# A row of attention scores spread by way of DRAM instead of by TensorE, in a four-layer graph network on one core

## The chip, the core and the metric

The kernel runs on one core of a Trainium2 chip. The time is the device time of the program in microseconds (us), the median of several runs. Names of engines: PE is TensorE (PEld its weight loads), DVE is VectorE, ACT is ScalarE, POOL is GpSimd, SP is SyncE, which here only issues transfers.

## The reference

There are 32 graphs with 512 nodes of 256 features, and an adjacency matrix of 512 x 512 for each. Four layers follow one another; each normalises x, applies a relu, runs one kind of graph attention and adds the result to x. Layers 1 and 2 are the ones that matter here. In both, the score of a pair of nodes is a sum of two numbers, one for each node:

```python
h = maximum(layernorm(x), 0)
# layer 1                                     # layer 2
Wh  = h @ W.T                                 Hh = h @ W
src = Wh @ a1 ; dst = Wh @ a2                 s = Hh @ a_src ; d = Hh @ a_dst
e = leaky_relu(src[:, None] + dst[None, :])   e = exp(-leaky_relu(s[:, None] + d[None, :]))
e = where(adj > 0, e, -9e15)                  e = where(adj != 0, e, 0)
x = x + softmax(e) @ Wh                       x = x + elu(e @ Hh / rowsum(e))
```

Layer 0 has scores q h^T and two products with the attention matrix, layer 3 a full bilinear score. Their code is not touched.

## The kernel before

A graph's 512 nodes lie as four tiles of 128 partitions (NT = 4, P = 128), its 256 features as two halves (HC = 2). Attention matrices are held transposed, in the tile eT: the node that is attended to (j) in the partitions, the node that attends (i) along the row, so that a product with the values needs no further transpose.

In layers 1 and 2, `scored_values` computes the values of each tile t and the two scores of its nodes in one product on PE (L488, with two extra columns of weights). DVE copies the two scores into sd (L492) and ACT the values into v (L495). Node t * 128 + p then has its scores in sd[p, 0, t] and sd[p, 1, t]. `leaky_exp_t` builds eT: it needs the first score of all 512 nodes as a row, the same row in every partition. It gets it with four transposes on PE (L509), one for each tile: the column sd[:, 0, t], broadcast over 128 columns and turned, is a block of 128 columns of row, which is one bank of PSUM. ACT then adds the second score as a bias and applies the leaky relu (L513, four times), and the exponential (L517, four times). DVE masks (L649 in layer 1, L684 in layer 2), and `attend` multiplies with the values on PE (L536).

At the start of a layer, `normed` normalises (DVE L407, GpSimd L414, ACT L421), splits the bits into planes (DVE L427), turns the planes with DMA transposes on SyncE (L432), and ACT joins the result to hT (L436), the operand of L488 and of the feature products L463. SyncE also loads x (L193) and adj (L200) and turns the codes made from adj (L389) and a small tile of layer 3 (L753). GpSimd stores the result (L833).

The order of all of this is written out beforehand by the class `Plan`. Every operation is entered with an engine, a cost (how long it holds its engine, and when its result is there), what it waits for, and the places that it takes or reads (8 banks of PSUM, a few buffers). `order` plays the graphs through on these costs: an engine that is free takes, of its ready operations, the one with the lowest rank. The rank is the number of the graph times a distance, less the length of the chain still ahead inside the graph. The distance is `APART` for all graphs, and for the last two steps between graphs `APART_LAST`. The instructions are emitted in the order that comes out, and every engine's queue runs in that order. Four graphs are in flight (`FLIGHT` = 4): graph b uses the tiles of graph b - 4 and begins when that one has been stored.

The tile row takes a bank. The tiles fa, zT and r share one buffer in each slot, one after another: fa and zT in layer 0, r in layer 2, fa again in layer 3.

Of the kernel before, what the change touches and what calls it, by code (L numbers as in the profile page):

```python
# [11 lines left out]
F32 = mybir.dt.float32  # L12
# [3 lines left out]
AF = mybir.ActivationFunctionType  # L16
# [3 lines left out]
P = 128  # L20
EPS = 1e-5
ALPHA = 0.2
# [10 lines left out]
def pe(n512=0, n256=0, nt=0):  # L33
    t = n512 * PE512 + n256 * PE256 + nt * PET
    return t, t + 170.0
# [4 lines left out]
A_COPY, A_HALF, A_PRELU, A_EXP, A_TANH = (477.0, 597.0), (253.0, 373.0), (570.0, 693.0), (519.0, 640.0), (373.0, 474.0)  # L40
A_BIAS, A_PRELU2 = (570.0, 687.0), (629.0, 722.0)
G_POW, G_STORE = (800.0, 850.0), (900.0, 900.0)
A_NORM, A_JOIN, V_SPLIT = (491.0, 590.0), (620.0, 767.0), (332.0, 422.0)
D_TURN = (1310.0, 2600.0)
D_X, D_ADJ, D_ADJ0 = (550.0, 5000.0), (550.0, 12000.0), (550.0, 2500.0)
G_LOAD = (800.0, 5000.0)


class Plan:
# [5 lines left out]

    PASS = 200.0

    APART, APART_LAST = 40000.0, 10000.0
    SLACK = {"V": (1.05, 0.0), "A": (1.05, 0.0), "G": (1.5, 0.0), "D": (1.0, 800.0)}

    def __init__(self):
# [2 lines left out]
    def op(self, engine, cost, after, emit, graph, takes=(), reads=()):  # L64


        much, more = self.SLACK.get(engine, (1.0, 0.0))
        cost = cost[0] * much, cost[1] * much + more
        flat = []
        for a in after:  # L70
            flat += a if isinstance(a, tuple) else [a]
        o = {"engine": engine, "cost": cost, "after": [a for a in flat if a is not None], "emit": emit,
             "graph": graph, "takes": takes, "reads": reads, "number": len(self.ops), "way": 0.0}
        for r in reads:
            r["readers"] += 1
        self.ops.append(o)
        return o

    @staticmethod
    def place(pool):  # L80

        return {"pool": pool, "readers": 0}

    def order(self, pools):
        free = {pool: list(range(n)) for pool, n in pools.items()}
        users = {}
        for o in self.ops:
            o["left"] = len(o["after"])
            for a in o["after"]:
                users.setdefault(a["number"], []).append(o)  # L90
        last = max(o["graph"] for o in self.ops)
        for o in reversed(self.ops):
            o["way"] += o["cost"][1] + self.PASS
            late = max(0, o["graph"] - last + 2)
            o["rank"] = ((o["graph"] - late) * self.APART + late * self.APART_LAST - o["way"], o["number"])
            for a in o["after"]:
                if a["graph"] == o["graph"]:
                    a["way"] = max(a["way"], o["way"])
        engines = sorted({o["engine"] for o in self.ops})
        ready = {e: [] for e in engines}  # L100
        at = dict.fromkeys(engines, 0.0)
        events = []
        numbers = itertools.count()
        for o in self.ops:
            if not o["left"]:
                heapq.heappush(ready[o["engine"]], (o["rank"], o))
        now, out = 0.0, []
        while True:
            for e in engines:
                skipped = []  # L110
                while at[e] <= now and ready[e]:
                    rank, o = heapq.heappop(ready[e])
                    need = [p["pool"] for p in o["takes"]]
                    if any(len(free[n]) < need.count(n) for n in need):
                        skipped.append((rank, o))
                        continue
                    for p in o["takes"]:
                        p["number"] = free[p["pool"]].pop(0)
                    holds, until = o["cost"]
                    at[e] = now + holds  # L120
                    out.append(o)
                    heapq.heappush(events, (at[e], next(numbers), None))
                    heapq.heappush(events, (now + until + self.PASS, next(numbers), o))
                for x in skipped:
                    heapq.heappush(ready[e], x)
            if not events:
                break
            now = events[0][0]
            while events and events[0][0] <= now:
                o = heapq.heappop(events)[2]  # L130
                if o is None:
                    continue
                for r in o["reads"]:
                    r["readers"] -= 1
                    if not r["readers"]:
                        free[r["pool"]].append(r["number"])
                for w in users.get(o["number"], []):
                    w["left"] -= 1
                    if not w["left"]:
                        heapq.heappush(ready[w["engine"]], (w["rank"], w))  # L140
        assert len(out) == len(self.ops), "the plan is stuck"
        return out, now
# [3 lines left out]
def kernel(  # L146
# [30 lines left out]
    nc = tc.nc  # L177
    B, N, H = x.shape
    NT = N // P
    HC = H // P  # L180
    FLIGHT = 4
# [3 lines left out]
    work = ctx.enter_context(tc.tile_pool(name="work", bufs=1))  # L185
    big = ctx.enter_context(tc.tile_pool(name="big", bufs=2))
    turns = ctx.enter_context(tc.tile_pool(name="turns", bufs=1))
    ps = ctx.enter_context(tc.tile_pool(name="ps", bufs=1, space=PSUM))


# [32 lines left out]
    plan = Plan()  # L223
# [76 lines left out]
    a = [load_rows(l1_sb, l1_w)]  # L300
# [4 lines left out]
    a = [load_rows(l2_aug, l2_w)]  # L305
    a = ready["l2"] = a + transposed(l2_aug[:, :, :H], l2_wt, a)
    a = a + [load_column(l2_ac, l2_a.rearrange("o n -> (o n)"))]
# [3 lines left out]
    t = transposed(l3_sb, wt3, [load_rows(l3_sb, l3_w)])  # L311
    a = product(lambda d: awt[:, d, :], a12_sb, lambda c: wt3[:, c, :], H, t + [load_rows(a12_sb, l3_a12)])
# [9 lines left out]
    for i in range(FLIGHT):  # L322
# [5 lines left out]
    rows, cols, pair, stat = [P, NT, N], [P, HC, N], [P, NT, H], [P, NT]  # L328
    KINDS = {
        "code": (rows, BF16, "code", 1), "codeT": (rows, BF16, "codeT", 1), "mask": (rows, BF16, "mask", 1),  # L330
        "eT": (rows, F32, "eT", 1), "hT": (cols, F32, "hT", 1),
        "fa": (cols, F32, "fa", 1), "zT": (cols, F32, "fa", 1), "r": (pair, F32, "fa", 1),
        "xn": (pair, F32, "y", 2), "y": (pair, F32, "y", 2), "z": (pair, F32, "y", 2), "w": (pair, F32, "y", 2),
        "crest": ([P, 4, N], BF16, "y", 2),
        "st": ([P, NT, 6], F32, "st", 2), "mv": ([P, NT, 2], F32, "mv", 2), "sd": ([P, 2, NT], F32, "sd", 2),
# [6 lines left out]
    def graph(b, before, code_before, x_before):  # L342


        slot = b % FLIGHT
# [12 lines left out]
        T = Tiles()  # L358

        def op(engine, cost, after, emit, takes=(), reads=()):  # L360
            return plan.op(engine, cost, after, emit, b, takes, reads)
# [29 lines left out]
        turned, code, rows_code = [], None, plan.place("code")  # L391
        for g in range(NT // 2):
            code = op("V", V_CODE, begin + [got_adj[2 * g + 2], code], partial(classes, g), takes=[] if code else [rows_code])
# [108 lines left out]
        def leaky_exp_t(l, ss, sign):  # L502


            place = plan.place("bank")

            def spread(t):
                p = bank(f"row{l}", place) if t == 0 else T[f"row{l}"]
                nc.tensor.transpose(p[:, t * P : (t + 1) * P],  # L509
                                    T[f"sd{l}"][:, 0, t : t + 1].to_broadcast([P, P]), ident)  # L510

            def leaky(c):
                nc.scalar.activation(T[f"eT{l}"][:, c, :], T[f"row{l}"], AF.Prelu, bias=T[f"sd{l}"][:, 1, c : c + 1], alpha=ALPHA)  # L513

            def exp(c):
                e = T[f"eT{l}"][:, c, :]
                nc.scalar.activation(e, e, AF.Exp, scale=sign)  # L517

            a = None
            for t in range(NT):  # L520
                a = op("PE", pe(nt=1), [ss[t], a], partial(spread, t), takes=[] if a else [place])
            ls = [op("A", A_PRELU, [a], partial(leaky, c), reads=[place]) for c in range(NT)]
            return [op("A", A_EXP, [x], partial(exp, c)) for c, x in enumerate(ls)]

        def attend(l, es, vs, use):
# [24 lines left out]
        for g in range(NT // 2):  # L550
            place = plan.place("bank")
# [12 lines left out]
            a = op("PE", pe(n256=8), hs[two(g)], partial(values, g, place), takes=[place])  # L564
            vs += [op("V", V_ADD, [a], partial(biased_v, g, j), reads=[place]) for j in range(2)]
        es = []
        for c in range(NT):
            place = plan.place("bank")
# [14 lines left out]
            a = op("PE", pe(n512=4), qs, partial(similar, c, place), takes=[place])  # L583
            a = op("A", A_COPY, [a] + (prepared if FLIGHT - 2 <= b < FLIGHT else []), partial(exp0, c), reads=[place])
# [24 lines left out]
        places_z, a = places, None  # L609
        for c in range(NT):  # L610
            a = op("PE", pe(n512=4), [ys[c], a], partial(again, c), takes=[] if c else places)
        zs = [op("A", A_COPY, [a], partial(evacuate_z, k), reads=[places[k]]) for k in range(HC)]
        xs = []
        for g in range(NT // 2):
            place = plan.place("bank")
# [19 lines left out]
            a = op("PE", pe(n256=8), zs + ready["w1"], partial(second_conv, g, place), takes=[place])  # L635
# [202 lines left out]
    for b in range(B):  # L838
        end, code, got_x = graph(b, ends[b - FLIGHT] if b >= FLIGHT else None, code, got_x)
        ends.append(end)  # L840
    order, took = plan.order({"bank": 8, "code": 1, "planes": 4, "planesT": 4})
    with tc.manual_schedule():
        for o in order:
            o["emit"]()
# [32 lines left out]
```

## The time and the profile before

| | |
|---|---|
| time, median of 3 runs | 2523.16 us (2522.11 to 2524.68) |
| span in the profile | 2520.1 us |
| PE, DVE, ACT, POOL busy | 98%, 66%, 65%, 11% |
| transposes for the row (L509) | 256 matmuls of 272 ns on average |
| leaky relu that reads it (L513) | 256 of 688 ns, 165.8 us in all |
| transfers issued by SyncE | 704 DMA transposes, 128 loads of adj, 32 loads of x |
| granted clock of TensorE | 0.997 |

Busy times of matmuls overlap one another, as the next begins before the last has ended; the sum of their durations is more than PE's busy time. How far apart they start is seen in the timeline.

### The profile page before, as it was taken

The page shows a single profiled execution, that of the slowest core. Times are in us where ns is not written, and L with a number is a line of the kernel's source. Part 1 is how long each engine was busy: PE and PEld are TensorE (multiplying, and loading weights), DVE is VectorE, ACT ScalarE, POOL GpSimd, SP SyncE. Part 2 cuts the span into 40 slices and gives each one's busy share as a digit, 9 for nine tenths or more (in the row PEclk, how much of TensorE's full clock was granted, in tenths as well). Part 3 has the DMA queues.
Part 4 walks back from the last instruction along what each step waited for, and adds up shares of the span by engine and source line. Part 5 has one row for each costly group of instructions (what it writes and reads, how often), then busy time and mean ns, then how long its engine had stood idle before and what let it go on. Part 6 is the DMA issues. An engine that isn't in the chain of part 4 may idle for free.

```text
span 2520.1 us, 30623 instructions
## 1 busy us (share of the span) xinstructions
PE 2482.1 (98%) x9532; PEld 1778.7 (71%) x9532; DVE 1674.4 (66%) x5106; ACT 1627.2 (65%) x3105; POOL 265.2 (11%) x314
## 2 busy tenths in 40 slices
PE   7999999999999999999999999999999999999998
PEld 5677777767777767777677777677776777767676
DVE  4467776666776667766667766677666677657476
ACT  4467776666666666666666666666666666657574
POOL 2001111011110001110111100011101111001000
PEclk9999999999999999999999999999999999999999
DMA  6123322222222322222232212322222332122111
GB/s 163 42 66 77 80 67 59 55 72 74 72 63 47 70 76 72 65 58 54 72 74 72 63 51 66 75 72 65 59 53 71 74 74 63 49 61 51 26 44 41
DMA packets 424499, 164.07 MB, mean 65 GB/s; under 512 B 386352, under 2 KB 403376, under 8 KB 424336
## 3 DMA queue, kind: packets, MB, share of 16 engines
q1 hardware_dynamic: 418304, 142.71, 24.4%
q0 software_dynamic: 5344, 18.75, 2.3%
q8 instruction: 76, 1.25, 0.2%
q14 instruction: 87, 0.71, 0.1%
q10 hardware_dynamic: 688, 0.66, 0.1%
HBM read 52.96 MB, written 16.78 MB: 28 GB/s over the span
## 4 chain that ended last, share of the span: by engine, by line
PE 94%; issue 3%; DVE 1%; ACT 1%; DMA 0%; POOL 0%; SPq 0%; POOLq 0%
PE av L536 34%; PE vp L488 13%; PE qk L573 9%; PE zp L603 9%; PE fp L463 8%; PE gk L731 8%; PE vp L558 4%; PE op L622 4%; PE hw L792 4%; PE row L509 1%; DMA x<-in_x_dram 0%; ACT eT L513 0%; PE wpp L274 0%; DVE st L407 0%; DVE mv L408 0%
## 5 line engine op out<-in xcount | busy, mean ns | idle before, releaser
L536 PE MATMUL av<-v,eT 128*128 128x257 f32 x4096 | 959.3, 381 | 12.0 <-DVE eT L649 7.4
L536 PEld LDWEIGHTS av<-v,eT 128*128 128x128 f32 x4096 | 775.3, 190 | 208.4 <-issue 100.8
L414 POOL TENSOR_TENSOR rstd<-ve,mhalf 128x2 f32<-128x2 f32 x256 | 230.5, 901 | 2044.0 <-DVE ve L411 1964.6
L436 ACT COPY hT<-planesT 128x512 uint16<-128x512 uint16 x512 | 384.7, 773 | 75.9 <-DMA planesT<-planes 74.2
L488 PE MATMUL vp<-l_aug,hT 128*128 128x258 f32 (+1 forms) x1536 | 378.5, 381 | 1.3 <-ACT hT L436 1.2
L488 PEld LDWEIGHTS vp<-l_aug,hT 128*128 128x128 f32 x1536 | 292.1, 191 | 81.0 <-issue 34.4
L495 ACT COPY v<-vp 128x256 f32<-128x256 f32 x384 | 139.7, 373 | 283.1 <-PE vp L488 263.3
L421 ACT ACTIVATE xn<-x,off,rstd 128x256 f32<-128x256 f32 x512 | 291.2, 608 | 32.8 <-DVE off L417 32.5
L492 DVE COPY sd<-vp 128x2 f32<-128x2 f32 (+1 forms) x384 | 60.3, 159 | 350.2 <-ACT v L495 249.1
L427 DVE COPY planes<-xn 128x512 uint16<-128x512 uint16 x512 | 212.4, 422 | 105.6 <-ACT xn L421 100.9
L603 PE MATMUL zp<-eT,y 128*128 128x512 f32 x512 | 240.5, 592 | 0.0
L573 PE MATMUL qk<-fa,hT 128*128 128x512 f32 x512 | 233.9, 592 | 0.0
L731 PE MATMUL gk<-hT,fa 128*128 128x512 f32 x512 | 225.4, 592 | 0.0
L407 DVE BATCH_NORM_STATS2 st<-x 128x6 f32<-128x256 f32 x512 | 210.0, 410 | 8.5 <-DMA x<-in_x_dram 7.6
L513 ACT ACTIVATE eT<-row,sd 128x512 f32<-128x512 f32 x256 | 165.8, 688 | 42.8 <-PE row L509 42.7
L731 PEld LDWEIGHTS gk<-hT,fa 128*128 128x128 f32 x512 | 97.3, 190 | 108.0 <-issue 99.5
L573 PEld LDWEIGHTS qk<-fa,hT 128*128 128x128 f32 x512 | 93.0, 190 | 89.6 <-issue 84.6
L517 ACT ACTIVATE eT<-eT 128x512 f32<-128x512 f32 x256 | 155.5, 638 | 0.0
L603 PEld LDWEIGHTS zp<-eT,y 128*128 128x128 f32 x512 | 96.6, 189 | 72.5 <-issue 65.6
L577 ACT ACTIVATE eT<-qk 128x512 f32<-128x512 f32 x128 | 77.2, 608 | 99.0 <-PE qk L573 98.9
L558 PE MATMUL vp<-w_sb,hT 128*128 128x256 f32 x512 | 121.7, 381 | 0.0
L463 PE MATMUL fp<-hT,att_sb 128*128 128x512 f32 x256 | 120.1, 594 | 1.5 <-DVE l_u L278 1.1
(95 smaller groups left out, 2899.2 us busy)
## 6 DMA issues: line engine op xcount, KB each, us to landing
adj<-in_adj_dram SPq DMA_DIRECT2D x128, 256.0 KB, 2.9
x<-in_x_dram SPq DMA_DIRECT2D x32, 512.0 KB, 4.1
out_dram<-y POOLq DMA_DIRECT2D x32, 512.0 KB, 3.7
planesT<-planes SPq DMA_TRANSPOSE x512, 2.3
codeT<-code SPq DMA_TRANSPOSE x128, 2.8
crest<-crest SPq DMA_TRANSPOSE x64, 2.4
spare<-in_L_gnn_W_dram POOLq DMA_DIRECT2D x2, 256.0 KB, 7.5
l_aug<-in_L_gnn_W_dram POOLq DMA_DIRECT2D x2, 256.0 KB, 6.4
```

The lines of the kernel that those rows point to most:

```text
L407: nc.vector.bn_stats(T[f"st{l}"][:, t, :], T["x"][:, t, :])
L414: nc.gpsimd.tensor_tensor(T[f"rstd{l}"][:, two(g)], T[f"ve{l}"][:, two(g)], mhalf[:, two(g)], ALU.pow)
L421: nc.scalar.activation(T[f"xn{l}"][:, t, :], T["x"][:, t, :], AF.Relu, bias=T[f"off{l}"][:, t : t + 1], scale=T[f"rstd{l}"][:, t : t + 1])
L427: nc.vector.tensor_copy(p, bits)
L436: nc.scalar.copy(bits[:, :, :, t * P : (t + 1) * P], T[f"planesT{l}{t}"].rearrange("p (b c) n -> p b c n", b=2))
L463: nc.tensor.matmul(p, w_sb[:, c, k * P : (k + 1) * P], T[f"hT{l}"][:, c, :], start=(c == 0), stop=(c == HC - 1))
L488: nc.tensor.matmul(p[:, :cols], T[f"hT{l}"][:, c, t * P : (t + 1) * P], w_aug[:, c, :], start=(c == 0), stop=(c == HC - 1))
L536: nc.tensor.matmul(p[:, : H + 1], T[f"eT{l}"][:, c, t * P : (t + 1) * P], v[:, c, :], start=(c == 0), stop=(c == NT - 1))
L558: nc.tensor.matmul(p[:, j * H : (j + 1) * H], T["hT0"][:, c, t * P : (t + 1) * P], w0_sb[:, c, :], start=(c == 0), stop=(c == HC - 1))
L573: nc.tensor.matmul(p, T["hT0"][:, k, c * P : (c + 1) * P], T["fa0"][:, k, :], start=(k == 0), stop=(k == HC - 1))
L603: nc.tensor.matmul(p, T["y0"][:, c, k * P : (k + 1) * P], T["eT0"][:, c, :], start=(c == 0), stop=(c == NT - 1))
L731: nc.tensor.matmul(p, T["fa3"][:, k, c * P : (c + 1) * P], T["hT3"][:, k, :], start=(k == 0), stop=(k == HC - 1))
```

## The change

For graphs 4 to 27 the row no longer passes through PE. SyncE writes the 128 x 4 scores to a small tile in DRAM, waits until they are there, and reads them back with a stride of zero over the partitions, so that all 128 get the same 512 numbers. The row now lies in SBUF, in the buffer of fa, zT and r, and in the order p * 4 + t instead of t * 128 + p; the leaky relu reads it with a step of four elements, so that eT keeps its order. The first four and the last four graphs keep the transposes. Two new costs tell the plan of the transfers. Apart from that, the plan no longer has one fixed pair of distances: it is played through for 17 values of `APART` from 34000 to 50000 and five of `APART_LAST` from 2000 to 14000, and the pair with the earliest planned end is used. The purpose is to take work off PE.

```diff
+D_OUT, D_SPREAD = (550.0, 3500.0), (550.0, 4500.0)
...
-    APART, APART_LAST = 40000.0, 10000.0
+    APART, APART_LAST = [1000.0 * k for k in range(34, 51)], [1000.0 * k for k in range(2, 15, 3)]
...
+    def best(self, pools):
+        apart = min(itertools.product(self.APART, self.APART_LAST), key=lambda a: self.order(pools, *a)[1])
+        return self.order(pools, *apart)
...
-            o["rank"] = ((o["graph"] - late) * self.APART + late * self.APART_LAST - o["way"], o["number"])
+            o["rank"] = ((o["graph"] - late) * apart + late * apart_last - o["way"], o["number"])
...
+    dram = ctx.enter_context(tc.tile_pool(name="dram", bufs=2, space=bass.MemoryType.DRAM))
...
-        "fa": (cols, F32, "fa", 1), "zT": (cols, F32, "fa", 1), "r": (pair, F32, "fa", 1),
+        "fa": (cols, F32, "fa", 1), "zT": (cols, F32, "fa", 1), "r": (pair, F32, "fa", 1), "row": (cols, F32, "fa", 1),
...
+            turned = b < FLIGHT or b >= B - FLIGHT
             place = plan.place("bank")
 
-            def spread(t):
+            def turn(t):
                 p = bank(f"row{l}", place) if t == 0 else T[f"row{l}"]
                 nc.tensor.transpose(p[:, t * P : (t + 1) * P],
                                     T[f"sd{l}"][:, 0, t : t + 1].to_broadcast([P, P]), ident)
 
+            def collect():
+                T[f"line{l}"] = d = dram.tile([P, NT], F32, tag=f"row_{slot}", name=f"row{l}_{b}")
+                nc.sync.dma_start(out=d, in_=T[f"sd{l}"][:, 0, :])
+
+            def spread():
+                d = T[f"line{l}"]
+                nc.sync.dma_start(out=T[f"row{l}"][:, 0, :],
+                                  in_=bass.AP(tensor=d.tensor, offset=d.offset, ap=[[0, P], [1, N]]))
+
             def leaky(c):
-                nc.scalar.activation(T[f"eT{l}"][:, c, :], T[f"row{l}"], AF.Prelu, bias=T[f"sd{l}"][:, 1, c : c + 1], alpha=ALPHA)
+                if turned:
+                    row = T[f"row{l}"].rearrange("q (t p) -> q t p", t=NT)
+                else:
+                    row = T[f"row{l}"][:, 0, :].rearrange("q (p t) -> q t p", t=NT)
+                nc.scalar.activation(T[f"eT{l}"][:, c, :].rearrange("q (t p) -> q t p", t=NT), row, AF.Prelu,
+                                     bias=T[f"sd{l}"][:, 1, c : c + 1], alpha=ALPHA)
...
-            for t in range(NT):
-                a = op("PE", pe(nt=1), [ss[t], a], partial(spread, t), takes=[] if a else [place])
-            ls = [op("A", A_PRELU, [a], partial(leaky, c), reads=[place]) for c in range(NT)]
+            if turned:
+                for t in range(NT):
+                    a = op("PE", pe(nt=1), [ss[t], a], partial(turn, t), takes=[] if a else [place])
+            else:
+                a = op("D", D_OUT, ss, collect)
+                a = op("D", D_SPREAD, [a], spread)
+            ls = [op("A", A_PRELU, [a], partial(leaky, c), reads=[place] if turned else []) for c in range(NT)]
...
-    order, took = plan.order({"bank": 8, "code": 1, "planes": 4, "planesT": 4})
+    order, took = plan.best({"bank": 8, "code": 1, "planes": 4, "planesT": 4})
```

The changes to the counting of readers in `op` and `place`, left out here, only let `order` be run more than once.

More of the change, by code (lines that the diff above doesn't have):

```diff
@@ L73, in op @@
              "graph": graph, "takes": takes, "reads": reads, "number": len(self.ops), "way": 0.0}
-        for r in reads:
-            r["readers"] += 1
         self.ops.append(o)
@@ L80, in place, with order @@
     def place(pool):
-        return {"pool": pool, "readers": 0}
-    def order(self, pools):
+        return {"pool": pool}
+    def best(self, pools):
+        apart = min(itertools.product(self.APART, self.APART_LAST), key=lambda a: self.order(pools, *a)[1])
+        return self.order(pools, *apart)
+    def order(self, pools, apart, apart_last):
         free = {pool: list(range(n)) for pool, n in pools.items()}
@@ L87, in order @@
         for o in self.ops:
-            o["left"] = len(o["after"])
+            o["left"], o["way"] = len(o["after"]), 0.0
+            for r in o["reads"]:
+                r["readers"] = 0
             for a in o["after"]:
                 users.setdefault(a["number"], []).append(o)
+        for o in self.ops:
+            for r in o["reads"]:
+                r["readers"] += 1
         last = max(o["graph"] for o in self.ops)
```

## The prediction

> **What bounds the kernel now.** I read the page from the top: busy shares first, then the slices, to see whether one engine is full all the time or only on average.
>
> ```profile
> PE 2482.1 (98%) x9532; PEld 1778.7 (71%) x9532; DVE 1674.4 (66%) x5106; ACT 1627.2 (65%) x3105; POOL 265.2 (11%) x314
> ...
> PE   7999999999999999999999999999999999999998
> ...
> PE 94%; issue 3%; DVE 1%; ACT 1%; DMA 0%; POOL 0%; SPq 0%; POOLq 0%
> ```
>
> TensorE is full in 38 of 40 slices and the chain that ended last lies on it. A modelled busy time can flatter TensorE, so I checked it with stretches one period long, and with the list of waits of PE over the whole run.
>
> ```profile
> 300.00:376.90 76.90, 76.90 (x297) 54.93 (x296) 52.50 (x158) 50.87 (x98) 8.19 (x9) 1.00 0.33 69
> 1000.00:1076.90 76.90, 76.90 (x297) 55.13 (x296) 52.45 (x159) 50.73 (x97) 8.18 (x9) 1.00 0.26 66
> ...
> ```
>
> (Columns: stretch, length, then busy us of PE, PEld, DVE, ACT, POOL, granted clock, DMA share, GB/s.) One graph takes one such stretch: the stores of two neighbours stand at 1047.30 and 1124.21 us, and all stores between 355 and 2124 us are 76.90 to 76.91 apart. PE waits for nothing between 200 and 2300 us; its nine waits all lie in the head and the tail. So in the steady part a graph costs exactly what its matmuls take, 76.905 us, while DVE (52.5) and ACT (50.8) have a third of the time free. Next, the operation that the change removes, by its tile and then in the timeline of PE:
>
> ```profile
> L509 PE MATMUL row<-ident,sd x256: 271/272/323, 86.5 to 2429.5; 128*128 128x128 f32 x128
> ...
> 1018.35 0.27 PE L509 MATMUL row<-ident,sd 128*128 128x128 f32 x1
> 1018.46 1.89 PE L792 MATMUL hw<-l_w1s,hT 128*128 128x256 f32 x8
> 1020.18 1.89 PE L622 MATMUL op<-w_sb,zT 128*128 128x256 f32 x8
> 1021.91 0.27 PE L509 MATMUL row<-ident,sd 128*128 128x128 f32 x1
> 1022.02 1.89 PE L622 MATMUL op<-w_sb,zT 128*128 128x256 f32 x8
> ```
>
> The trap is in the first line: 256 x 0.272 us would be 69.6 us. That is a latency. In the timeline the next matmul starts 0.11 us after the transpose (1018.35 to 1018.46, 1021.91 to 1022.02), so 0.11 us is what it costs a full PE. Matmuls with 512 columns start 0.43 us apart (four in 1.72 us), and 128 columns are a quarter of that, 0.1075 us; I use this. Check of the pitches: av 128 x 0.2168, the L488 products 10.43 in all, qk, zp, gk and fp 64 x 0.43, vp, op and hw 48 x 0.2156, eight transposes 0.86: 76.9 us, the measured period. No other cost hides beside them.
>
> Last, the stores of the end, because the change alters the plan there too:
>
> ```profile
> 2306.74 0.79 POOL L833 DMA_DIRECT2D out_dram<-y  x1 [6.40 <-DVE y L822]
> 2424.13 0.79 POOL L833 DMA_DIRECT2D out_dram<-y  x1 [7.05 <-DVE y L822]
> ...
> 2515.28 0.75 POOL L833 DMA_DIRECT2D out_dram<-y  x1 [7.02 <-DVE y L822]
> ```
>
> The store at 2306.74 is graph 27's and lets the last graph begin in its slot; that graph ends at 2515.28, after 209 us, with three others beside it. In the steady part a graph has four periods, 308 us. So some 100 us of its stay are waiting for a turn, and a longer chain inside a graph can use them.
>
> [...] DMA transposes land after 2.3 to 2.8 us, adj tiles after 2.9, stores to DRAM after 3.7. [...]
>
> **The change part by part.** *Removed:* four transposes for each of layers 1 and 2 of graphs 4 to 27: 24 x 8 = 192 of 256. All stand in the part where PE never waits, so their pitch comes off the end: 192 x 0.1075 = 20.6 us (period 76.905 - 0.86 = 76.045 us). Their weight loads go too, beside it.
>
> *Added on the queues:* two transfers a layer, 96 in all, on SyncE. Per graph SyncE now issues 22 transposes of 1.21 us and five loads of about 0.57, 29.5 of 76.9 us. Four more issues make 31.8 us. The write out (2 KB in pieces of 16 bytes) is in no row: [...] the 3.7 us of a store the upper; I take 2.5. The spread (128 rows of 2 KB, 256 KB) is nearest to an adj tile, same size and direction: 2.9 us, up to the 9.3 us of the b_sb broadcast in the crowded start; I take 3.5. So SyncE can stand for 2.5 us twice a graph with transposes of planes and code and the loads of adj queued behind it. ACT L436, and through it PE L488 and L463, wait for those transposes. The plan charges the pair 3.5 + 4.5 us with 0.8 us of slack and 0.2 us of passing for each, 10.0 us, and puts other work there; my 6 us lie within. The 48 spreads move 12.6 MB more in a run whose DMA engines are 26 to 33% busy: hidden beside PE.
>
> *The longer chain:* from the scores to ACT L513 it was under 1 us, now 6 [...], twice a graph[...]. They fit into the 100 us of waiting above. Cost nothing, hidden beside the matmuls of the three other graphs.
>
> *ACT:* L513 now reads the row from SBUF in steps of 16 bytes. Nearest row for an awkward access: L436, which writes at a stride, 773 ns against 593 for the plain copy L468, 0.18 us more. Lower bound none (688 from PSUM)[...]. I take 0.2: eight a graph, 1.6 us [...] on 50.8 of ACT's 76. Hidden beside PE, as ACT does not reach it.
>
> *Moved:* a bank of PSUM is free for some 10 us twice a graph; PE lacks none, so nothing. The row sits in the tile of fa, zT and r, whose readers are done before and whose next writer comes after L513, so no new wait that lasts. The first and last four graphs keep their transposes: nothing there.
>
> *The distances:* the plan tries 17 x 5 pairs and keeps the one that its own costs end soonest. The middle cannot gain (PE full), only the idle time of PE in head and tail: 11.1 and 4.2 us for weights at the start are fixed by loads, and what an order could touch is 1.1 + 0.2 + 2.3 in the head and 1.2 + 4.2 + 0.3 + 0.4 + 3.2 + 2.2 in the tail, 15 us. The best order by the costs need not be the best on the chip. I put this at nothing, with up to 15 us down and some 8 up.
>
> Sum: 2523.2 - 20.6 = 2502.6; I say 2502.5 us.
>
> **The rivals.** *Slower: the transfers starve TensorE.* SyncE's order is fixed, so a late write out holds transposes up, ACT gets no hT, PE stops. The break-even is 20.6 / 48 = 0.43 us of lost PE time for each spread; at 1 us it would be 2502.5 + 48 = 2550.5 us. For it: 76 waits of ACT L436 for planesT already sum to 74.2 us. Against it: none of them reaches PE in the middle, and SyncE has 45 us a graph to spare.
>
> *The scalar engine or SyncE shows through in part.* With ACT at its upper cost and the spread slow, the planned order is late now and then and PE waits 0.2 us a spread: +10 us, 2512.5 us. [...] Against it: ACT has 26 us a graph free.
>
> *The ends get shorter as well.* Half of the 15 us idle: 2495 us. For it: in the tail PE waits 4.2 us for eT of layer 1 and 3.2 us for another, which a different distance may fill. Against it: it is picked by estimates.
>
> **How the numbers follow.** Forecast (2498 to 2508) 0.62; shorter ends (below 2498, about 2495) 0.12; partly exposed (2508 to 2518, about 2512.5) 0.14; no change within 5 us 0.03; slower, 2550.5, 0.09. The range reaches from most of the shorter ends to most of the partly exposed, 2491 to 2515: it leaves out 0.03 below and about 0.15 above. Faster by over 0.2% is below 2518.1: 0.62 + 0.12 + 0.14 = 0.88; same 0.03; slower 0.09.
>
> **What would show it.** Right: stores of the middle 76.04 to 76.05 us apart, no wait of PE between graph 4 and 27, 64 matmuls left on the row; DMA issues of 48 writes and 48 spreads with landings under 4 us each; ACT up by less than 3 us a graph. Wrong: PE waits for eT of layers 1 or 2 or for hT in the middle; SyncE waiting several us at the spread with planesT late behind it; a period above 76.1; or middle as forecast and the difference in the idle time of PE before 250 and after 2280 us, which would be the distances.

## The result and the profile after

| | before | after |
|---|---|---|
| time, median of four runs | 2523.11 us (2522.11 to 2524.68) | 2495.44 us (2494.66 to 2496.24) |
| ratio | | 0.989, interval 0.9873 to 0.9907 |
| span in the profile | 2520.1 us | 2494.2 us |

The changed kernel is 27.7 us faster, 7 us more than the forecast and inside the range. The line numbers have moved: the relu that reads the row is now L538, the exponential L543, the transposes L521, the write out L526, the spread L530, the products with the values L566, the scores and values L498, the join to hT L446.

The page of the changed kernel, its busy shares and its chain by engine:

```profile
PE 2462.8 (99%) x9340; PEld 1762.9 (71%) x9340; DVE 1641.0 (66%) x5106; ACT 1720.9 (69%) x3105; POOL 257.8 (10%) x314
...
PE 93%; issue 2%; ACT 2%; DMA 1%; DVE 1%; POOL 0%; SPq 0%; POOLq 0%; DVEq 0%
```

The bound is the same. PE has 192 matmuls less; ACT is busy for 94 us more.

Stretches of the changed kernel, one new period of 76.05 us each (length, then busy us of PE, PEld, DVE, ACT, POOL; clock; DMA share; GB/s):

```profile
1000.00:1076.05 76.05, 76.05 (x290) 54.51 (x289) 50.88 (x159) 55.31 (x99) 7.96 (x9) 1.00 0.30 74
2000.00:2076.05 76.05, 76.05 (x290) 54.48 (x289) 51.75 (x158) 54.97 (x96) 7.75 (x9) 1.00 0.30 76
```

A graph takes 76.05 us of PE with no gap, as forecast (fourteen graphs between the stores at 510.74 and 1575.48 us: 1064.74 / 14 = 76.05). ACT went from 50.7 to 55 us a period.

The tile row of the changed kernel (least, median, longest ns), and its two transfers (KB, median us to landing):

```profile
L538 ACT ACTIVATE eT<-row,sd x256: 667/1222/1277, 93.3 to 2412.3; 128x512 f32<-128x512 f32 x128
L521 PE MATMUL row<-ident,sd x64: 271/272/322, 89.2 to 2406.6; 128*128 128x128 f32 x64
```

```profile
row<-row SPq DMA_DIRECT2D x48, 256.0 KB, 4.1
...
row<-sd SPq DMA_DIRECT2D x48, 2.0 KB, 1.6
```

The transfers take 5.7 us together, the 6 us that were forecast. The relu takes 1.22 us where it reads from SBUF with a step, against 0.69 where it read from PSUM: 0.53 us more, where I took 0.2.

Stores at the end of the changed kernel:

```profile
2269.37 0.79 POOL L863 DMA_DIRECT2D out_dram<-y  x1
2381.77 0.79 POOL L863 DMA_DIRECT2D out_dram<-y  x1 [3.53 <-DVE sd L502]
...
2489.30 0.75 POOL L863 DMA_DIRECT2D out_dram<-y  x1 [4.41 <-DVE y L852]
```

From the store of graph 25 (2123.99 before, 2110.57 now) to the end of the span it was 396.1 us and is 383.6: 12.5 us less. The last four graphs run the same instructions as before, and graphs 26 and 27, which are in work at that store, have together 1.7 us of transposes less at most. Up to the store of graph 3 it is 3.3 us more, between the two stores 16.7 less. So 9.2 of the 25.9 us by which the profile is shorter, about a third, do not lie in the steady part. The busy time of PE says the same: it is 19.3 us less (2482.1 to 2462.8), which is about what the transposes cost, and the time in which PE stands is 6.6 us less (38.0 to 31.4). Where these last us come from is what the experiments are about.

### The profile page after: what moved, and what is told of

It is laid out like the page before. It is cut to its first block, busy times and chain, and to the rows that moved or that the text cites. A ratio compares the mean times of both kernels' runs of the same rounds, so it can differ in the third digit from the quotient of the medians.

```text
span 2494.2 us, 30551 instructions
## 1 busy us (share of the span) xinstructions
PE 2462.8 (99%) x9340; PEld 1762.9 (71%) x9340; DVE 1641.0 (66%) x5106; ACT 1720.9 (69%) x3105; POOL 257.8 (10%) x314
## 4 chain that ended last, share of the span: by engine, by line
PE 93%; issue 2%; ACT 2%; DMA 1%; DVE 1%; POOL 0%; SPq 0%; POOLq 0%; DVEq 0%
PE av L566 34%; PE vp L498 13%; PE fp L473 9%; PE qk L603 9%; PE zp L633 9%; PE gk L761 8%; PE op L652 4%; PE vp L588 4%; PE hw L822 4%; DMA planesT<-planes 1%; DMA adj<-in_adj_dram 1%; ACT eT L538 1%; PE wpp L284 0%; ACT eT L543 0%; ACT xn L431 0%
## 5 line engine op out<-in xcount | busy, mean ns | idle before, releaser
L566 PE MATMUL av<-v,eT 128*128 128x257 f32 x4096 | 954.5, 381 | 5.1 <-DVE eT L714 2.2
L566 PEld LDWEIGHTS av<-v,eT 128*128 128x128 f32 x4096 | 772.0, 190 | 207.6 <-issue 90.4
L446 ACT COPY hT<-planesT 128x512 uint16<-128x512 uint16 x512 | 382.0, 764 | 148.8 <-DMA planesT<-planes 146.8
L424 POOL TENSOR_TENSOR rstd<-ve,mhalf 128x2 f32<-128x2 f32 x256 | 223.2, 914 | 1613.0 <-DVE ve L421 1563.2
L498 PE MATMUL vp<-l_aug,hT 128*128 128x258 f32 (+1 forms) x1536 | 371.5, 381 | 1.1 <-ACT hT L446 1.1
L498 PEld LDWEIGHTS vp<-l_aug,hT 128*128 128x128 f32 x1536 | 291.6, 190 | 73.1 <-issue 25.6
L431 ACT ACTIVATE xn<-x,off,rstd 128x256 f32<-128x256 f32 x512 | 277.6, 594 | 83.0 <-DVE off L427 82.8
L538 ACT ACTIVATE eT<-row,sd 128x512 f32<-128x512 f32 x256 | 269.5, 1096 | 16.1 <-PE row L521 16.0
L603 PE MATMUL qk<-fa,hT 128*128 128x512 f32 x512 | 239.3, 592 | 0.0
L505 ACT COPY v<-vp 128x256 f32<-128x256 f32 x384 | 131.7, 375 | 100.4 <-PE vp L498 93.8
L543 ACT ACTIVATE eT<-eT 128x512 f32<-128x512 f32 x256 | 154.0, 634 | 0.0
L714 DVE SCALAR_TENSOR_TENSOR eT<-codeT,eT 128x512 f32<-128x512 bf16 x128 | 87.4, 690 | 80.9 <-ACT eT L543 80.8
L849 ACT ACTIVATE r<-y,one 128x512 f32<-128x512 f32 x64 | 46.7, 730 | 131.6 <-DVE y L838 131.6
L765 DVE SCALAR_TENSOR_TENSOR eT<-gk,sd,mask 128x512 f32<-128x512 f32 x128 | 95.5, 748 | 57.6 <-PE gk L761 56.7
```

What stands on the lines that cost most here:

```text
L424: nc.gpsimd.tensor_tensor(T[f"rstd{l}"][:, two(g)], T[f"ve{l}"][:, two(g)], mhalf[:, two(g)], ALU.pow)
L431: nc.scalar.activation(T[f"xn{l}"][:, t, :], T["x"][:, t, :], AF.Relu, bias=T[f"off{l}"][:, t : t + 1], scale=T[f"rstd{l}"][:, t : t + 1])
L446: nc.scalar.copy(bits[:, :, :, t * P : (t + 1) * P], T[f"planesT{l}{t}"].rearrange("p (b c) n -> p b c n", b=2))
L498: nc.tensor.matmul(p[:, :cols], T[f"hT{l}"][:, c, t * P : (t + 1) * P], w_aug[:, c, :], start=(c == 0), stop=(c == HC - 1))
L538: nc.scalar.activation(T[f"eT{l}"][:, c, :].rearrange("q (t p) -> q t p", t=NT), row, AF.Prelu, bias=T[f"sd{l}"][:, 1, c : c + 1], alpha=A ...
L566: nc.tensor.matmul(p[:, : H + 1], T[f"eT{l}"][:, c, t * P : (t + 1) * P], v[:, c, :], start=(c == 0), stop=(c == NT - 1))
```

## The experiments

The runs were spread over three chips, and each ratio is to the kernel before on the same chip; its median there was 2525.66, 2526.63 and 2525.11 us.

**Is it the spread or the distances?** Three kernels take the change apart. The first keeps the transposes everywhere and takes the pair of distances that the plan then chooses:

```diff
-    APART, APART_LAST = [1000.0 * k for k in range(34, 51)], [1000.0 * k for k in range(2, 15, 3)]
+    APART, APART_LAST = [35000.0], [10000.0]
...
-            turned = b < FLIGHT or b >= B - FLIGHT
+            turned = True
```

> All 32 graphs keep the transposes; only the choice of distances is done, which without spreads falls on 35000 and 10000. Theory (the gain is 20.6 us of transposes in the middle, the other 7 us are ends that the distances shorten): period stays 76.905 us, time 2511 to 2520 us. Rival (the choice of distances did most of it): 2500 us or less.

Measured: 2508.12 us, ratio 0.9931 (0.9916 to 0.9946), a gain of 17.5 us with no row spread, and a period still of 76.90 to 76.92 us. That is more than the theory said (2511 to 2520 us) and less than the rival (2500 us or less).

The second is the same at the pair that the changed kernel uses:

```diff
+    APART, APART_LAST = [44000.0], [10000.0]
...
+            turned = True
```

> All graphs keep the transposes, at the distances 44000 and 10000 that the changed kernel picks. Theory (distances are worth 7 us in the ends): 2515 to 2518 us. Rival (distances alone are worth nothing, it is the pair that counts): 2521 to 2525 us.

Measured: 2513.84 us, ratio 0.9954 (0.9937 to 0.9971), a gain of 11.8 us, a little more than the theory said. Stores come in turns of 74.92 and 78.89 us, 76.905 on average: PE is as full as before, and all of it is in the ends. From 0.9954 to the changed kernel's 0.989 is another 16 us, which is the spread at these distances.

The third is the spread at the distances of before:

```diff
+    APART, APART_LAST = [40000.0], [10000.0]
```

> The spread alone, at the distances of before, 40000 and 10000. Theory: period 76.05 us and the ends of the kernel before, 2502 to 2504 us. Rival (the ends became shorter by the spread itself, a free bank or a freer PE): 2495 to 2497 us. Rival (the spread needs the right distances to stay hidden): PE waits in the middle, above 2508 us.

Measured: 2523.56 us, ratio 0.9992 (0.9986 to 0.9999). The operation that I had priced at 20.6 us gave 2. The last of the three expectations held: PE waits in the middle. Its waits between 460 and 1980 us (total us, times, longest), the chain of work around one of them (start, us, what), and PE and ACT there:

```profile
PE av L566 <- DVE x L734: 5.3, 9, 1.0
```

```profile
1040.13 1.11 ACT eT L538
1041.24 0.52 ACT eT L803
1041.76 0.52 ACT eT L543
1042.28 1.11 ACT eT L538
1043.39 0.49 ACT eT L607
1043.88 0.52 ACT eT L543
1044.40 2.28 ACT eT L538 x2
1046.68 0.53 ACT eT L543
...
1047.23 1.29 DVE eT L679 x2
...
1050.14 8.94 PE av L566 x40
```

```profile
1040.62 8.83 PE L566 MATMUL av<-v,eT 128*128 128x257 f32 x40
1050.14 8.94 PE L566 MATMUL av<-v,eT 128*128 128x257 f32 x40 [0.69 <-DVE x L734]
1058.91 3.62 PE L822 MATMUL hw<-l_w1s,hT 128*128 128x256 f32 x16
```

```profile
1048.89 0.84 ACT L727 ACTIVATE y<-av,rs 128x256 f32<-128x256 f32 x2 [1.17 <-DVE rs L722]
1049.62 0.84 ACT L730 ACTIVATE r<-av,rs 128x256 f32<-128x256 f32 x2
```

Read it from the bottom. PE is done at 1049.45 and goes on at 1050.14. It is not waiting for the masks, which were there at 1048.52 (L679). The product needs two banks of PSUM, and in the plan the old product av of layer 2 leaves its bank when ACT has read it for r (L730). The two reads end at 1050.10 and 1050.46, and in the trace the weight loads of PE at 1050.14 and 1050.51 wait on ACT's semaphore. The x of DVE that the list names (L734) ends at the same moment as the first read; for the second load PE waits for ACT alone. Behind the reads the chain goes on: y and r wait for rs of DVE (L722), rs stands in DVE's queue behind the masks, the masks wait for ACT, and in this chain ACT is full for 7.1 us, 4.5 of them the relu at 1.11 us from one start to the next. The other waits of the list show the same sequence. Over a quarter of ACT's time is free over the stretch (1101.90 of 1530 us are busy), but the order put eight relus between 1030 and 1047 us, at little more than half of what they take.

The period is 76.53 us on average over twenty stores (455.50 to 1986.02), 0.48 above the forecast. The list has 5.3 of these 10 us, as it counts from the end of a matmul; the rest sits at the same places. Forty products at 0.217 us take 8.68 us. To the next start it is 9.52 us for the first forty here and 8.77 for the second: 0.93 us lost where the list shows 0.69. Summed in the trace over the twenty periods, the starts of matmuls that come late there lose 10.2 us.

**Is it the read or the transfers?** First I tried to have the row come back in the order of the nodes, so that ACT needs no step, once at the changed kernel's distances and once at the old ones:

```diff
-                T[f"line{l}"] = d = dram.tile([P, NT], F32, tag=f"row_{slot}", name=f"row{l}_{b}")
-                nc.sync.dma_start(out=d, in_=T[f"sd{l}"][:, 0, :])
+                T[f"line{l}"] = d = dram.tile([NT, P], F32, tag=f"row_{slot}", name=f"row{l}_{b}")
+                nc.sync.dma_start(out=d.rearrange("t p -> p t"), in_=T[f"sd{l}"][:, 0, :])
...
-                    row = T[f"row{l}"][:, 0, :].rearrange("q (p t) -> q t p", t=NT)
+                    row = T[f"row{l}"][:, 0, :].rearrange("q (t p) -> q t p", t=NT)
```

> As the changed kernel, with the same plan, but the scores are written to DRAM tile by tile (512 pieces of 4 bytes), so the row comes back in the order of the nodes and the leaky relu reads it without a step. Theory (in the changed kernel the dear read is hidden beside PE): the relu falls from 1.22 to 0.65 to 0.69 us, the write lands later than its 1.6 us (2 to 4 us), period still 76.05 us, time within 3 us of the changed kernel, ratio to before 0.988 to 0.990. Rival (ACT's dear read costs time at the ends): ratio 0.985 or less. Rival (the small pieces are slow and hold SyncE up): above 0.992.

> The spread at the old distances 40000 and 10000 with the row in order, so ACT reads it without a step; the same plan as the spread alone, which gained 2 us. Theory (there ACT, late by the dear reads, makes PE wait in the middle): PE waits in the middle vanish, period 76.05 us, 10 us below the spread alone, ratio to before 0.994 to 0.996. Rival (it is the transfers' delay, not the read): ratio 0.998 to 1.000 and the waits stay.

Measured: 2728.06 us, ratio 1.0798 (1.078 to 1.0816), and 2796.67 us, ratio 1.1069 (1.105 to 1.1087). As a test of the read both failed, as they changed the write as well. As a test of a late transfer they are clear. The DMA issue and the waits of SyncE and PE in the first of the two:

```profile
row<-sd SPq DMA_DIRECT2D x48, 2.0 KB, 9.7
```

```profile
SPq L530 <- DMA row<-sd: 414.8, 47, 10.6
```

```profile
PE av L566 <- DVE eT L679: 76.9, 26, 4.5
PE vp L498 <- ACT hT L446: 59.2, 27, 3.5
```

The same 2 KB in pieces of 4 bytes land after 9.7 us and not 1.6. SyncE stands 8.8 us at each spread (56.2 us for all of them in the changed kernel), and PE waits both for masks of the late row and for hT. The chain before one of the waits for hT:

```profile
1010.53 10.60 DMA row<-sd
...
1021.14 3.74 DMA row<-row
...
1024.90 1.33 ACT eT L538 x2
1026.23 0.66 ACT hT L446
...
1026.94 4.65 PE vp L498 x12
```

The planes for hT were not late: ACT waits for planesT 141.9 us in this run and 146.8 in the changed kernel. The copy to hT stands in ACT's queue behind two relus of the late row, for which ACT waits 233.3 us in all. So PE stops as in the first rival of the prediction, but by way of ACT's queue and not of the transposes on SyncE. One transfer that lands 8 us later puts the kernel (1.0798 - 0.989) x 2526.63 = 229 us above the changed one, 4.8 for each spread. Not all of it is waiting: the granted clock was 0.967 over this run and 0.997 over the changed one. At the old distances PE waits 215.5 us for the masks of layer 2.

The clean test leaves the transfers alone and leaves out the sorting:

```diff
+    APART, APART_LAST = [40000.0], [10000.0]
...
-                    row = T[f"row{l}"][:, 0, :].rearrange("q (p t) -> q t p", t=NT)
+                    row = T[f"row{l}"][:, 0, :].rearrange("q (t p) -> q t p", t=NT)
```

> The spread at the old distances 40000 and 10000, same plan and same transfers as the spread alone, but the relu reads the row as it comes back, without the step of four; the sorting of the row is left out, so each score stands at another node. Theory (in the spread alone the dear read makes ACT late and PE wait): relu 0.65 to 0.70 us, no wait of PE between 460 and 1980 us, period 76.05 us, 8 to 14 us below the spread alone, ratio to before 0.993 to 0.996. Rival (the transfers' delay or the order itself): waits stay, ratio 0.998 or more.

Measured: 2503.96 us, ratio 0.9919 (0.9905 to 0.9932). The relu by its tile, and the stretch from 455 to 1985 us of this kernel and of the spread alone:

```profile
L538 ACT ACTIVATE eT<-row,sd x256: 676/708/745, 92.6 to 2416.3; 128x512 f32<-128x512 f32 x128
```

```profile
455.00:1985.00 1530.00, 1530.00 (x5793) 1098.84 (x5792) 1038.25 (x3207) 1029.75 (x1954) 148.00 (x184) 1.00 0.32 74
```

```profile
455.00:1985.00 1530.00, 1524.60 (x5759) 1090.37 (x5758) 1030.00 (x3180) 1101.90 (x1940) 144.80 (x180) 1.00 0.32 73
```

Same plan, same transfers, relu at 0.71 us: PE is full again, the period is 76.02 us, and the gain is 21 us, about the 20.6 that were counted for the transposes. The difference to the spread alone is (0.9992 - 0.9919) x 2525 = 18 us, more than the 8 to 14 that I expected. This shows that at the old distances it is the step in the read that took back the gain, and that the transfers cost nothing that can be measured there.

**Does a longer chain hide at any distance?** The spread at the pair of the first kernel:

```diff
+    APART, APART_LAST = [35000.0], [10000.0]
```

> The spread at distances 35000 and 10000, the pair that e1 takes for transposes. Theory (a graph waits 100 us of its 308 for its turn, so the longer chain stays hidden at any distance): period 76.05 us, 2495 to 2512 us. Rival (with graphs ranked closer together the longer chain is no longer filled by other graphs): PE waits in every period, slower than before, 2530 to 2690 us.

Measured: 2727.72 us, ratio 1.08 (1.0784 to 1.0816). The theory, my own step of 100 us of waiting, fell. Waits of PE and stretch between 455 and 1985 us:

```profile
PE vp L498 <- ACT hT L446: 101.4, 49, 3.1
```

```profile
455.00:1985.00 1530.00, 1412.68 (x5115) 974.06 (x5114) 917.51 (x2837) 985.60 (x1723) 115.19 (x162) 0.98 0.28 65
```

PE runs dry in every period (85 to 88 us from store to store), waiting for the start of a layer. The next kernel asks whose fault that is, the chip's 6 us or the order that the plan made for the 10 us that it charges (3.5 + 4.5 with slack and passing). With the measured delays the plan charges 1.7 + 4.3 us and the same 2 us on top, 8 in all:

```diff
-D_OUT, D_SPREAD = (550.0, 3500.0), (550.0, 4500.0)
+D_OUT, D_SPREAD = (430.0, 1700.0), (330.0, 4300.0)
...
+    APART, APART_LAST = [35000.0], [10000.0]
```

> The spread at 35000 and 10000 as in the run that took 2728 us, but the plan is told the delays that the profile of the changed kernel shows (1.7 and 4.3 us instead of 3.5 and 4.5). Theory (the 200 us were lost by the order that the plan made for a pair of transfers of 10 us, not by the chip's 6 us): ratio to before 0.99 to 1.01. Rival (the chip's own chain starves PE when graphs are ranked this close): ratio 1.03 or more.

Measured: 2526.12 us, ratio 0.9999 (0.9991 to 1.0007). The same instructions and the same pair, ordered for a shorter delay, take 200 us less. So the loss lay in the order. PE still idles for 15 us between 455 and 1985 us, mostly for a tanh of ACT, which the dear read may explain; this was not tried apart:

```profile
PE zp L633 <- ACT y L622: 13.2, 15, 1.9
```

**What does a transpose cost PE?** In the kernel before, each one done twice:

```diff
-                nc.tensor.transpose(p[:, t * P : (t + 1) * P],
-                                    T[f"sd{l}"][:, 0, t : t + 1].to_broadcast([P, P]), ident)
+                for _ in range(2 if FLIGHT <= b < B - FLIGHT else 1):
+                    nc.tensor.transpose(p[:, t * P : (t + 1) * P],
+                                        T[f"sd{l}"][:, 0, t : t + 1].to_broadcast([P, P]), ident)
```

> The kernel before with each transpose of graphs 4 to 27 done twice, the plan not told. Theory (a transpose costs a full PE its pitch of 0.1075 us): 192 more give 20.6 us, period 77.77 us, ratio to before 1.0075 to 1.0085. Rival (it costs its latency of 0.27 us): 52 us, ratio 1.02. Rival (it is hidden in gaps): ratio 1.000.

Measured: 2545.57 us, ratio 1.0078 (1.0063 to 1.0093), period 77.78 us. Eight transposes are worth 0.875 us, 0.109 each: the pitch (0.11 us in the timeline of before) and not the latency (0.27).

**Why are the first and last graphs left out?**

```diff
-            turned = b < FLIGHT or b >= B - FLIGHT
+            turned = False
```

> All 32 graphs are spread, with the distances that the plan then picks (44000 and 11000). Theory (in head and tail PE waits for chains, so the longer chain costs more than the 64 transposes at 0.1075 us give back, 6.9 us): 3 to 12 us slower than the changed kernel, ratio to before 0.990 to 0.994. Rival (PE's work counts there as well): 0.986 to 0.987.

Measured: 2537.7 us, ratio 1.0047 (1.0032 to 1.0062), slower than the kernel before. Not only the ends are longer: the order is another one in the middle too, and there PE waits for ACT. Its waits over the whole run:

```profile
PE qk L603 <- ACT r L730: 15.0, 24, 0.7
...
PE av L566 <- ACT eT L803: 5.8, 4, 2.8
```

Once in each period a bank is read late by ACT, and the period is 76.90 us, where it was before any transpose was removed. By the stores of graphs 3 and 25 (452.55 and 2144.49 us) the kernel loses 16.7 us to the changed one between the two, 17.2 before and 7.5 after. So the ends are 24.7 us longer and the theory of the ends explains no more than that, 6 tenths of the loss; whether the longer chain itself or the other pair of distances (44000 and 11000) does it there was not tried apart.

**A plan that knows the read.** The plan is told that the relu with the step holds ACT for 1.11 us, and is used at the pair that is then best by its costs:

```diff
+A_PRELU_STEP = (1110.0, 1225.0)
...
+    APART, APART_LAST = [48000.0], [6000.0]
...
-            ls = [op("A", A_PRELU, [a], partial(leaky, c), reads=[place] if turned else []) for c in range(NT)]
+            ls = [op("A", A_PRELU if turned else A_PRELU_STEP, [a], partial(leaky, c), reads=[place] if turned else []) for c in range(NT)]
```

> The changed kernel with the plan told what the dear read costs ACT (1.11 us of the engine, result after 1.225 us), at the pair that it then finds best, 48000 and 6000. Theory (what is left above the plan is ACT running late at the ends): period 76.05 us and shorter ends, 2 to 8 us below the changed kernel of the same call, ratio to before 0.985 to 0.988. Rival (the ends are bound by the graphs' own chains): the same as the changed kernel, 0.988 to 0.990.

> The changed kernel once more on the chip of this call, as the measure for the run with the dear read priced: ratio to before 0.988 to 0.990.

Measured: 2493.22 us (2489.82 to 2493.41), ratio 0.9871 (0.9858 to 0.9885), beside 2498.03 us (2496.06 to 2499.05), ratio 0.9891 (0.9876 to 0.9906), of the changed kernel on the same chip. All runs of the one lie below all of the other, 4.8 us by the medians, while the two intervals of the ratios still overlap. Its period is 76.01 us (76.04 in the changed kernel beside it), so most of the difference lies in the ends. The cost and the pair were changed together, and what each of them brings was not tried apart. It is the fastest version here.

## Why the prediction held, and where it did not

The measured time lies inside the range, but not in the case that I held likeliest. That was 2498 to 2508 us, at 0.62; what came is the rival "The ends get shorter as well", about 2495 us, at 0.12. It fits by its reason too: half of the 15 us of idle time was to go, and PE stands 6.6 us less in the whole run. The prediction names this outcome among its signs of being wrong: the middle as forecast, and the difference in the idle time of PE in head and tail.

- *PE bounds the middle, and a transpose costs 0.1075 us there.* Right: 76.05 us a graph as forecast, and 0.109 us by doubling them.
- *Write out and spread, 2.5 + 3.5 us.* Right in sum: 1.6 + 4.1. SyncE stood 1.2 us at a spread, less than I allowed. The 2.5 for the write was an estimate with no measured lower bound. The write landed in less than half of the 3.7 us of a store to DRAM, which was my upper bound.
- *"I put this at nothing", of the distances.* This is the term that was mis-sized. At the pair that the changed kernel takes, the distances alone are worth 11.8 us, and at the pair that suits the transposes 17.5. My bound of 15 us from PE's idle time was about right, only a little small; taking the middle of it for nothing was not. The idle time itself is not all: matmuls after one of the pauses were slower too. In the kernel before, after the wait of 4.2 us that ends at 2311.84 us, four of L536 took 2.05 us and not 1.03, and the granted clock from 2308.4 to 2315.2 us was 0.50.
- *The relu's read: 0.2 us, "hidden beside PE".* The size was 0.53, and ACT rose by 4 us a graph and not by less than 3. The second half is wrong as a statement about the kernel. It is hidden in the order of the changed kernel and costs 18 us in the order of before. My argument was an average, that ACT has 26 us a period free. In the spread alone the queue of ACT had over a quarter of its time free and was still full for 7.1 us in the chain shown, and PE waited at the end of that stretch, 0.69 us, for a bank that ACT emptied too late.
- *The longer chain: "They fit into the 100 us of waiting above. Cost nothing".* True in the changed kernel, wrong as a reason. At 35000 the order planned for 10 us of delay took 200 us more than the one planned for 8, with the same instructions.
- *The rival in which transfers starve PE.* It did not happen, but it is 8 us of landing away: with 9.7 us for the write it cost 4.8 us for each spread, through relus that stood in ACT's queue ahead of hT. The order decides as well: at 35000 PE ran dry with the transfers as they are.

So the forecast of the middle was right, and the extra 7 us came from the ends, where PE stands less at the new distances. That it held owes something to luck: without the new distances the spread gave 2 us. The part of the change that I had put at nothing decided whether the part that I had worked out would show.

## What to carry to other kernels

Where an order is fixed beforehand, price a removed operation on the full engine by its pitch (here 0.109 us, beside a latency of 0.27), and then ask whether the order still fits what replaces it: the same edit gave 21 us, 2 us or a loss of 200 us with nothing but the order or one read changed. A plan's costs for a new operation have to be measured and put in, in both directions, too long a delay as much as too short a read. And test the two halves of such a change apart, since their sum says little on either.

## What the runs showed of the hardware that I had not expected

- In the traces of the two kernels at 40000 and 10000, a relu of ACT that reads 512 f32 a partition from SBUF at a step of 16 bytes took 1.23 us (median), against 0.71 without the step, from the same tile and with the same plan: 0.52 us more.
- 2 KB written from 128 partitions to DRAM landed after 1.6 us in 128 pieces of 16 bytes (median of 48 in the changed kernel), and after 9.7 us in 512 pieces of 4 (median of 48 in the kernel with the row in order at the same distances).
- 256 KB spread from one line of 2 KB in DRAM landed after 4.1 us, against 3.0 for the same amount of adj, both medians of the changed kernel.
